# First loads, first splits and decay exponentials in another order, in a fused lightning-attention and router kernel

## The chip, the cores and the metric

The kernel runs on one core of a Trainium2 chip. The metric is the device time of one execution in microseconds (us), the median of three runs. A core has five engines with queues of their own: TensorE (PE in the profile; its weight loads are PEld), VectorE (DVE), ScalarE (ACT), GpSimd (POOL) and SyncE (SP), which here only issues DMAs. ACT issues some as well. Each engine takes its instructions strictly in the order in which the program lists them.

## The reference

Layer norm of x, a lightning-attention block s on it, a top-8 router block g on it, and x + s * silu(g). There are 2048 tokens of 512 features, read as four sequences of 512 by the kernel, 16 heads of 128, 64 experts.

```python
xn = _layernorm(x, axis=-1)
qkv = silu(einsum('bnf,of->bno', xn, w_qkv))       # q, k, v per head
q_decay = exp(-s * arr[:, None]); k_decay = exp(-s * (BLK - arr)[:, None])
diag_decay = where(idx >= 0, exp(-s * idx), 0.0);  block_decay = exp(-s * BLK)
# per block of tokens: o = (q * q_decay) @ kv + ((q k^T) * diag_decay) @ v
#                      kv = block_decay * kv + (k * k_decay)^T v
out = norm_w * (out * rsqrt(mean(out * out) + EPS))
s = einsum('bno,fo->bnf', sigmoid(einsum('bnf,of->bno', xn, w_gate)) * out, w_out)
logits = einsum('th,eh->te', flat, router_weight) + router_bias
topk_w, topk_idx = top_k(softmax(logits), 8)
g = silu(flat * sum(topk_w) + einsum('tk,tkh->th', topk_w, expert_bias[topk_idx]))
x = x + s * g
```

(`reshape` and the like are left out; `s` in the decays is the slope of the head.)

## The kernel before

**Tiles.** Tokens are cut into tiles of 128. The sequences go in two pairs p = 0, 1; a tile (p, t) means the t-th 128 tokens of both sequences of a pair, so two arrays x (128 x 512, float32). For each tile DVE takes mean and variance (`layer_norms`, L235: `bn_stats` L240, `bn_aggr` L241, add epsilon L242), POOL raises the variance to -1/2 (L246 or L250), DVE normalises in place (L216), PE transposes four 128 x 128 pieces per sequence into PSUM (`transpose`, L259), and the result is copied to `xf`.

**Split products.** Every large matrix product is done in float32r with operands split in two: a high half, which ACT casts (`split_hi`, L110), and a low half, source minus high half, which DVE or POOL subtracts (`split_lo`, L113). A product is three matmuls: high x high, high x low, low x high (`PASSES`). The products themselves follow a Strassen scheme with seven block products (`PRODUCTS`, L39): token blocks B11, B21, B22 and sums T1 to T4, weight blocks A11, A12, A22 and sums S1 to S4.

**The first stage.** It computes v for all heads in 16 units: `for k, (p, t) in enumerate(tiles + again)` (L1032), eight tiles with the first half of v's weights, `ws[0]`, then eight with `ws[1]`. Each is a `v_unit`. Units 0 and 1 are direct (`plain_unit`, L537): 8 block products of 6 matmuls, A11 with B11 and T1 (for a direct unit T1 holds the plain block b12), A12 with B21 and B22, then A21 and A22 with the same token blocks. The later ones use the Strassen scheme (`unit`, L498). A list `after` has seven places; what is put in place i is issued behind product i of the unit. In a direct unit, places 0, 1 and 2, 3 and 4, 5 and 6 come behind the products of A11, A12, A21 and A22. Through `after` a unit prepares the next tiles: `stats`, `norms`, `turn` (transposes, copies, and for p = 0 a store of `xf`), `sums`, `plain` and `more` (token blocks and their splits), `logits` (the router's 16 small matmuls, and one addition of the bias on DVE), and sums and splits of weights (`sum_of`, `split_one`).

**The start** is written out by hand (L985 to L1030). SP issues the loads: two x of tile (0,0), four weight blocks of `ws[0]`, two x of tile (0,1), four more weight blocks (`raw_v`, 256 KB each; two blocks make one of A11, A12, A21, A22). ACT issues five small loads (slope twice, router weight, router bias, norm weight) behind a table load for Exp. POOL makes the identity, and the distances for the decays (`make_dist`, L167). PE does `WARM` = 32 transposes of the identity. Then `make_decays` (L179): three exponentials on ACT and a memset on POOL. ACT loads the table for Silu (L1008). Then come the stats and norms of tile (0,0), its transposes, and the splits of unit 0 in the order of L1013 to L1030:

```python
pt = [transpose(stage, 0, j, 0, False) for j in range(PB)]
nc.vector.tensor_copy(xfs[0, 0][:, 0], pt[0])
split_hi(blocks[0, "B11"][:, 0, 0], pt[0][:, 0:KC])
ws[0].split_one("A11", nc.vector, hi=True)
```

with `logits(stage, 0, 0, [0])`, the router's matmuls for the first sequence, ahead of unit 0, and those of the second behind its first product.

**The decays** are made by row (`decay_row`), stored to DRAM by `keep_rows` (at unit 2) and spread to 128 partitions by `keep_decay`, one DMA per head, in units 13 to 15. The router's scores are exponentiated on ACT in unit 13 (`scores_exp`, L351). The attention behind the first stage reads both.

**Behind the first stage** come the units of gate and of q and k with the attention, the output projection and the final sum. The change touches nothing there.

PSUM: the transposes and the router's sums share a pool `ps_sc` of three banks, taken in turn.

Of the kernel before, what the change touches and what calls it, by code (L numbers as in the profile page):

```python
# [8 lines left out]
F32 = mybir.dt.float32  # L9
F32R = mybir.dt.float32r  # L10
AF = mybir.ActivationFunctionType
ALU = mybir.AluOpType
# [7 lines left out]
TOP_K = 8  # L20
LN_EPS = 1e-05
RMS_EPS = 1e-06
WARM = 32

# [36 lines left out]
def kernel(  # L61
# [44 lines left out]
    def tok(b, t):  # L106
        return bass.ds(b * N + t * P, P)
# [71 lines left out]
    def make_decays():  # L179
        nc.scalar.activation(decay_row, decay_row, AF.Exp, scale=slope_of)  # L180
        nc.scalar.activation(kdecay, slopes, AF.Exp, scale=rest_of)
        nc.scalar.activation(bdecay, slopes, AF.Exp, scale=-float(P))
        nc.gpsimd.memset(decay_row[:, 0 : P - 1], 0.0)

    def keep_rows():
# [40 lines left out]

    xts = {}

    def load_x(stage, b, t, bufs=None):
        xt = stage.tile([P, F], F32, tag="x", name=f"x_{b}_{t}", bufs=bufs)  # L230
        nc.sync.dma_start(out=xt, in_=x[tok(b, t), :])
        xts[b, t] = xt


    def layer_norms(p, t, apart=False):  # L235
        var = small.tile([P, PB], F32, tag="lnvar", name=f"lnv_{p}_{t}")
        for j in range(PB):
            b = p * PB + j
            st = small.tile([P, nc.vector.BN_STATS_DIM], F32, tag="bn", name=f"bn_{b}_{t}")
            nc.vector.bn_stats(st, xts[b, t])  # L240
            nc.vector.bn_aggr(stats[b][:, t, :], st)  # L241
            nc.vector.tensor_scalar(  # L242
                var[:, j : j + 1], stats[b][:, t, 1:2], 1.0, LN_EPS, ALU.mult, ALU.add
            )
            if apart:
                nc.gpsimd.tensor_tensor(  # L246
                    rstd_of[p][:, t, j : j + 1], var[:, j : j + 1], mhalf[:, 0:1], ALU.pow
                )
        if not apart:
            nc.gpsimd.tensor_tensor(rstd_of[p][:, t], var, mhalf[:, 0:PB], ALU.pow)  # L250
# [669 lines left out]
    NP_FIRST = 2  # L920

    def prepare(stage, p, t):
        first = (p, t) == (0, 0)
# [12 lines left out]
        def route_logits():  # L936
            logits(stage, p, t)
        return {
            "stats": lambda: layer_norms(p, t, first), "norms": lambda: normalise_x(p, t),
            "turn": turn, "sums": sums[0], "plain": sums[1], "more": sums[2], "logits": route_logits,  # L940
        }

# [39 lines left out]
    n1 = len(tiles)  # L982
    prep = [prepare(stage, p, t) for p, t in tiles]

    load_pair(stage, 0, 0)  # L985
    vloads = ws[0].load()
    vloads(4)
    load_pair(stage, 0, 1)
    vloads(4)
    make_first()  # L990

    nc.scalar.activation(kdecay[:, 0:NT], mhalf, AF.Exp)
    nc.scalar.dma_start(out=slope_of, in_=slope.rearrange("o h -> h o"))
    nc.scalar.dma_start(out=slopes, in_=slope.to_broadcast([P, NH]))
    nc.scalar.dma_start(out=rw, in_=router_w)
    nc.scalar.dma_start(out=rb, in_=router_b.to_broadcast([P, E]))
    nc.scalar.dma_start(out=nw, in_=norm_w)
    make_dist()
    sig = small.tile([P, NT], F32, tag="var", name="table")
    warm_up(WARM)  # L1000
    for i, n in enumerate(XN):
        block(0, i, xa if i < NX else xb, i)
        blocks[1, n] = blocks[0, n]
    for n in ["A21"] + [n for n, _, _, _ in PRODUCTS]:
        ws[0].place(n)
    make_decays()

    nc.scalar.activation(sig, mhalf, AF.Silu)  # L1008
    prep[0]["stats"]()
    prep[0]["norms"]()  # L1010

    pt = [transpose(stage, 0, j, 0, False) for j in range(PB)]
    nc.vector.tensor_copy(xfs[0, 0][:, 0], pt[0])  # L1013
# [12 lines left out]
    prep[1]["stats"]()  # L1026
    prep[1]["norms"]()
    ws[0].split_one("A21", nc.vector)
    load_pair(stage, *tiles[3])
    ws[0].split_one("A22", nc.gpsimd)  # L1030

    for k, (p, t) in enumerate(tiles + again):  # L1032
        g, after = k // n1, nothing()
        for unit_of, what in ((n1 - 3, (0, "top")), (n1 - 2, (0, "less")), (n1 + 2, (1, "top")), (n1 + 3, (1, "less"))):
            if k == unit_of:
                after[2].append(lambda what=what: scores_less(*what))
        if n1 - NT <= k < n1:
            after[6].append(lambda p=p, t=t: keep_blocks(p, t))
        if k + 1 < n1:
            after[0 if k else 1].append(prep[k + 1]["turn"])  # L1040
            if 0 < k < n1 - 3:
                after[0].append(lambda k=k: load_pair(stage, *tiles[k + 3]))
            if k == 0:
                after[1].insert(0, prep[2]["stats"])
            after[1].append(prep[k + 1]["sums"])
            if k + 2 < n1:
                if k:
                    after[1].append(prep[k + 2]["stats"])
                after[4 if k > 1 else 3].append(prep[k + 2]["norms"])
            after[1].append(prep[k + 1]["plain"])  # L1050
# [305 lines left out]
```

## Time and profile before

| what | value |
|---|---|
| median of 3 runs | 1055.41 us (1055.09 to 1055.75) |
| profiled execution, whole | 1056.31 us |
| its span (first to last instruction) | 1054.5 us |
| DVE, ACT, POOL busy | 638.3, 553.4, 682.0 us |
| granted TensorE clock | 1.00 throughout |
| DMA over the span | 185.12 MB, mean 176 GB/s |
| first warm-up transpose / first transpose of x | 1.38 / 7.39 us |
| first product of unit 0 / of unit 1 | 9.97 / 26.89 us |
| `scores_exp` in unit 13: table load / next Silu table load | 161.48 / 165.66 us |

Read the span as the time between the first and the last instruction; the execution's own time is some 1.8 us longer. "Busy" is the time in which an engine has an instruction of its own running; a wait shows as idle time before the instruction that waited, with the one that released it. SPq and ACTq lines are the issuing of DMAs, not the transfers.

### The profile page before, as it was taken

What the parts mean: (1) busy time and instruction counts of PE and PEld (TensorE: products, weight loads), DVE (VectorE), ACT (ScalarE), POOL (GpSimd) and SP (SyncE); (2) the same over time, 40 slices, a digit from 0 to 9 for tenths busy, and PEclk for the clock granted to TensorE, in tenths of its full rate; (3) what the DMA queues carried; (4) which work ended last, traced back from release to release, by engine and by line L of the source; (5) the groups of instructions that cost most, each with busy time, mean ns of one, the idle gap of its engine ahead of it and who ended that gap; (6) DMA issues with size and microseconds to landing.
All of it is one profiled execution on the core that took longest, in us unless ns stands there. A gap on an engine that the chain in (4) does not pass through costs nothing.

```text
span 1054.5 us, 17612 instructions
## 1 busy us (share of the span) xinstructions
PE 1044.0 (99%) x6338; PEld 925.0 (88%) x6338; DVE 638.3 (61%) x1017; ACT 553.4 (52%) x969; POOL 682.0 (65%) x698
## 2 busy tenths in 40 slices
PE   8999999999999999999999999999999999999997
PEld 7888888888888888888888888888888889999997
DVE  6675533347677676665554555555555458698767
ACT  5555554645545545555554555555545545574632
POOL 4887782768678777786777778877678643024023
PEclk9999999999999999999999999999999999999999
DMA  6456746544455455553854323633334236988863
GB/s 226 166 205 237 272 148 223 173 129 151 140 166 193 132 170 169 158 179 105 305 192 139 119 76 105 192 94 115 103 114 145 65 136 237 335 300 299 286 218 102
DMA packets 128838, 185.12 MB, mean 176 GB/s; under 512 B 11104, under 2 KB 72688, under 8 KB 127856
## 3 DMA queue, kind: packets, MB, share of 16 engines
q1 hardware_dynamic: 127856, 183.56, 53.1%
q8 instruction: 50, 0.82, 0.3%
q10 hardware_dynamic: 896, 0.44, 0.1%
q14 instruction: 36, 0.29, 0.1%
HBM read 115.26 MB, written 70.80 MB: 176 GB/s over the span
## 4 chain that ended last, share of the span: by engine, by line
PE 90%; DVE 4%; DMA 3%; ACT 1%; issue 1%; SPq 1%; POOL 0%; DVEq 0%; ACTq 0%; POOLq 0%
PE u_qk L516 27%; PE u_g L516 15%; PE u_v L516 13%; PE acc L1235 12%; PE sa L672 5%; PE o L757 5%; PE ss L695 4%; PE o L759 4%; PE kt L675 2%; PE d_v L546 1%; DMA raw_v<-in_w_v_dram 1%; PE lg L332 1%; DMA yin<-y 1%; ACT yr L110 1%; DMA raw_eb<-in_expert_b_dram 1%
## 5 line engine op out<-in xcount | busy, mean ns | idle before, releaser
L1235 PE MATMUL acc<-wr,yr 128*128 128x256 f32 x1344 | 163.4, 282 | 1.3 <-DVE a_o L900 1.3
L1235 PEld LDWEIGHTS acc<-wr,yr 128*128 128x128 f32 x1344 | 161.4, 190 | 3.3 <-DVE a_o L900 1.7
L516 PE MATMUL u_qk<-blk_T,ws_qk 128*128 128x512 f32 x576 | 141.6, 394 | 0.0
L769 POOL TENSOR_TENSOR sqs<-sqs,sq 128x512 f32<-128x512 f32 x60 | 79.1, 1318 | 94.9 <-ACT sq L768 94.9
L516 PEld LDWEIGHTS u_qk<-blk_T,ws_qk 128*128 128x128 f32 x576 | 107.0, 188 | 22.6
L113 POOL TENSOR_TENSOR ws_qk<-sum_qk,ws_qk 128x512 fp32r<-128x512 f32 x64 | 84.7, 1335 | 29.8 <-ACT ws_qk L110 29.8
L516 PE MATMUL u_qk<-blk_B,wa_qk 128*128 128x512 f32 x384 | 102.0, 401 | 0.0
L880 POOL TENSOR_TENSOR u<-u,x 128x256 f32<-128x256 f32 x28 | 33.4, 1213 | 99.5 <-DVE u L879 76.6
L113 DVE TENSOR_TENSOR yr<-yin,yr 128x1024 fp32r<-128x1024 f32 x56 | 75.6, 1354 | 35.5 <-ACT yr L110 35.4
L560 ACT ACTIVATE k<-k 128x512 f32<-128x512 f32 x64 | 40.5, 632 | 106.3 <-DVE k L507 106.3
L757 PE MATMUL o<-at,vin 128*128 128x128 f32 x512 | 88.5, 275 | 0.0
L516 PEld LDWEIGHTS u_qk<-blk_B,wa_qk 128*128 128x128 f32 x384 | 69.5, 189 | 14.5 <-ACT q L560 1.1
L110 ACT CAST yr<-yin 128x1024 fp32r<-128x1024 f32 x56 | 58.3, 1045 | 43.9 <-PE acc L1235 34.4
L761 DVE SCALAR_TENSOR_TENSOR y<-o,nw,gt 128x512 f32<-128x512 f32 x64 | 48.0, 751 | 49.9 <-PE o L759 49.9
L757 PEld LDWEIGHTS o<-at,vin 128*128 128x128 f32 x512 | 74.9, 192 | 2.5
L759 PE MATMUL o<-qd,st 128*128 128x128 f32 x384 | 74.3, 275 | 0.0
L768 ACT ACTIVATE sq<-o 128x512 f32<-128x512 f32 x60 | 35.9, 598 | 72.9 <-POOL sqs L769 41.7
L681 ACT ACTIVATE kd<-kt,kdecay 128x384 f32<-128x384 f32 x64 | 37.2, 581 | 67.9 <-PE kt L675 67.9
L516 PE MATMUL u_g<-blk_T,ws_g 128*128 128x512 f32 x288 | 72.4, 397 | 0.0
L699 DVE SCALAR_TENSOR_TENSOR st<-st,bdecay,ss 128x128 f32<-128x128 f32 x128 | 41.7, 346 | 44.2 <-ACT st L697 41.9
L672 PE MATMUL sa<-q,k 128*128 128x128 f32 x512 | 67.9, 276 | 0.3
L672 PEld LDWEIGHTS sa<-q,k 128*128 128x128 f32 x512 | 64.4, 191 | 3.8 <-ACT k L560 0.6
(199 smaller groups left out, 2405.6 us busy)
## 6 DMA issues: line engine op xcount, KB each, us to landing
yin<-y SPq DMA_DIRECT2D x56, 512.0 KB, 4.5
v<-vo_v SPq DMA_DIRECT2D x64, 256.0 KB, 2.8
raw_qk<-in_w_head_dram SPq DMA_DIRECT2D x64, 256.0 KB, 4.2
vin<-v SPq DMA_DIRECT2D x64, 256.0 KB, 3.6
y<-yS SPq DMA_DIRECT2D x64, 256.0 KB, 3.5
y<-y SPq DMA_DIRECT2D x48, 256.0 KB, 2.4
woin<-wo SPq DMA_DIRECT2D x18, 512.0 KB, 5.2
x<-in_x_dram SPq DMA_DIRECT2D x32, 256.0 KB, 4.6
```

The source lines that it names most:

```text
L110: nc.scalar.copy(hi, src)
L113: eng.tensor_tensor(lo, src, hi.bitcast(F32), ALU.subtract)
L516: nc.tensor.matmul(ps, lhsT, rhs, start=(first and c == 0 and n == 0), stop=(c == KC - 1 and n == len(PASSES) - 1), skip_group_check=not f ...
L560: nc.scalar.activation(dst, src, AF.Silu)
L672: nc.tensor.matmul(pa[:, c], k[:, c], q[:, c], start=True, stop=True)
L695: nc.tensor.matmul(ps[:, c], kd[s][:, c], v_of(b, h, c), start=True, stop=True)
L699: nc.vector.scalar_tensor_tensor(r[:, c], r[:, c - 1], bdecay[:, h : h + 1], ps[:, c], ALU.mult, ALU.add)
L757: nc.tensor.matmul(o, v_of(b, h, c), at[s][:, c], start=True, stop=(c == 0))
L759: nc.tensor.matmul(o, st[s][:, c - 1], qd[s][:, c - 1], start=False, stop=True)
L761: nc.vector.scalar_tensor_tensor(y, po, nw[:, h : h + 1], gts[s], ALU.mult, ALU.mult)
L769: nc.gpsimd.tensor_tensor(sq[b], sq[b], s1, ALU.add)
L1235: nc.tensor.matmul(acc[t // 2][:, t % 2], yr[:, yi, bass.ts(t, P)], wos[m, g // NQ][:, wi, g % NQ], start=(first and g == 0 and n == 0 and ...
```

## The change

- **Loads.** The second x of tile (0,0) is issued on ACT's queue. SP issues the first x, all eight weight blocks, the two x of tile (0,1), the router's weight and bias, and behind the first splits the slope loads and the norm weight. The x of tile (0,2) goes ahead of the store of `xf`.
- **Exponentials.** `make_decays` moves to unit 13, right ahead of `scores_exp`; its memset becomes `mask_decays`, in place 2 of that unit with `keep_rows`. The table load for Exp at the start goes. `keep_decay` starts two places later.
- **Start.** 24 warm-up transposes instead of 32, and the six others between the transposes of the two sequences. Stats, power and normalise of the two sequences are interleaved (`bn_of`). Splits are issued by halves of a weight block, in another order; A22's second low half goes from POOL to DVE.
- **Unit 0.** Tile (0,1)'s transposes and blocks and tile (0,2)'s stats move from place 1 to place 3, and all of tile (0,0)'s router matmuls to place 6.

```diff
-WARM = 32
+WARM = 24
...
+    def mask_decays():
         nc.gpsimd.memset(decay_row[:, 0 : P - 1], 0.0)
...
+    def load_x(stage, b, t, bufs=None, queue=None):
         xt = stage.tile([P, F], F32, tag="x", name=f"x_{b}_{t}", bufs=bufs)
+        (queue or nc.sync).dma_start(out=xt, in_=x[tok(b, t), :])
...
+    def bn_of(b, t):
+        p, j = b // PB, b % PB
+        st = small.tile([P, nc.vector.BN_STATS_DIM], F32, tag="bn", name=f"bn_{b}_{t}")
+        var = small.tile([P, PB], F32, tag="lnvar", name=f"lnv_{b}_{t}")
+
+        def power(j):
+            nc.vector.bn_aggr(stats[b][:, t, :], st)
+            nc.vector.tensor_scalar(
+                var[:, j : j + 1], stats[b][:, t, 1:2], 1.0, LN_EPS, ALU.mult, ALU.add
+            )
+            nc.gpsimd.tensor_tensor(
+                rstd_of[p][:, t, j : j + 1], var[:, j : j + 1], mhalf[:, 0:1], ALU.pow
+            )
+        return lambda: nc.vector.bn_stats(st, xts[b, t]), power
...
-    load_pair(stage, 0, 0)
-    vloads = ws[0].load()
-    vloads(4)
+    load_x(stage, 0, 0)
+    load_x(stage, 1, 0, queue=nc.scalar)
+    ws[0].load()(8)
     load_pair(stage, 0, 1)
-    vloads(4)
     make_first()
 
-    nc.scalar.activation(kdecay[:, 0:NT], mhalf, AF.Exp)
-    nc.scalar.dma_start(out=slope_of, in_=slope.rearrange("o h -> h o"))
-    nc.scalar.dma_start(out=slopes, in_=slope.to_broadcast([P, NH]))
-    nc.scalar.dma_start(out=rw, in_=router_w)
-    nc.scalar.dma_start(out=rb, in_=router_b.to_broadcast([P, E]))
-    nc.scalar.dma_start(out=nw, in_=norm_w)
+    sig = small.tile([P, NT], F32, tag="var", name="table")
+    nc.scalar.activation(sig, mhalf, AF.Silu)
+    nc.sync.dma_start(out=rw, in_=router_w)
+    nc.sync.dma_start(out=rb, in_=router_b.to_broadcast([P, E]))
     make_dist()
...
-    make_decays()
-
-    nc.scalar.activation(sig, mhalf, AF.Silu)
-    prep[0]["stats"]()
-    prep[0]["norms"]()
-
-    pt = [transpose(stage, 0, j, 0, False) for j in range(PB)]
+
+    first = [bn_of(b, 0) for b in range(PB)]
+    first[0][0]()
+    first[0][1](0)
+    first[1][0]()
+    normalise(xts[0, 0], xts[0, 0], 0, 0)
+    first[1][1](1)
+    pt = [transpose(stage, 0, 0, 0, False)]
+    warm_up(6)
     nc.vector.tensor_copy(xfs[0, 0][:, 0], pt[0])
+    normalise(xts[1, 0], xts[1, 0], 1, 0)
+    pt.append(transpose(stage, 0, 1, 0, False))
...
-    split_hi(blocks[0, "B11"][:, 0, 0], pt[0][:, 0:KC])
-    ws[0].split_one("A11", nc.vector, hi=True)
-    split_lo(nc.gpsimd, blocks[0, "B11"][:, 0, 1], b11, blocks[0, "B11"][:, 0, 0])
...
+    weights_hi("A11", 0)
+    tokens_hi("B11", pt[0][:, 0:KC])
+    weights_hi("A11", 1)
+    tokens_lo("B11", b11, nc.gpsimd)
+    weights_lo("A11", 0, nc.vector)
+    weights_lo("A11", 1, nc.vector)
+    weights_hi("A12", 0)
     nc.scalar.copy(xfs[0, 0][:, 1], pt[1])
+    load_pair(stage, *tiles[2])
     nc.sync.dma_start(out=xf_d[0], in_=xfs[0, 0])
-    load_pair(stage, *tiles[2])
-    warm_up(6)
-    split_blocks(0, 0, nc.vector, (("T1", b12), ("B21", b21), ("B22", b22)))
-    ws[0].split_one("A12", nc.vector, 0)
-    ws[0].split_one("A12", nc.gpsimd, 1)
-    logits(stage, 0, 0, [0])
+    tokens_hi("T1", b12)
+    tokens_lo("T1", b12, nc.vector)
+    tokens_hi("B21", b21)
+    weights_hi("A12", 1)
+    weights_lo("A12", 0, nc.vector)
+    weights_lo("A12", 1, nc.gpsimd)
+    tokens_lo("B21", b21, nc.vector)
+    tokens_hi("B22", b22)
+    tokens_lo("B22", b22, nc.vector)
+    ws[0].split_one("A21", nc.vector)
+    for i in range(2):
+        weights_hi("A22", i)
+    weights_lo("A22", 0, nc.gpsimd)
     prep[1]["stats"]()
+    weights_lo("A22", 1, nc.vector)
     prep[1]["norms"]()
-    ws[0].split_one("A21", nc.vector)
+    nc.sync.dma_start(out=slope_of, in_=slope.rearrange("o h -> h o"))
+    nc.sync.dma_start(out=slopes, in_=slope.to_broadcast([P, NH]))
+    nc.sync.dma_start(out=nw, in_=norm_w)
     load_pair(stage, *tiles[3])
-    ws[0].split_one("A22", nc.gpsimd)
...
         if k + 1 < n1:
-            after[0 if k else 1].append(prep[k + 1]["turn"])
+            early = 1 if k else 3
+            after[0 if k else 3].append(prep[k + 1]["turn"])
...
             if k == 0:
-                after[1].insert(0, prep[2]["stats"])
-            after[1].append(prep[k + 1]["sums"])
+                after[3].insert(0, prep[2]["stats"])
+            after[early].append(prep[k + 1]["sums"])
...
+            after[early].append(prep[k + 1]["plain"])
...
+            if k == 0:
+                after[6].append(lambda: logits(stage, 0, 0))
             after[4 if k else 6].append(prep[k + 1]["logits"])
-        if k == 0:
-            after[0].append(lambda: logits(stage, 0, 0, [1]))
...
-        if k == NP_FIRST:
-            after[0].append(keep_rows)
+        if k == n1 + NT + 1:
+            after[1] += [make_decays, scores_exp]
+            after[2] += [mask_decays, keep_rows]
         if n1 + NT < k < n1 + 2 * NT:
             for j in range(1, len(PRODUCTS)):
-                h = (k - n1 - NT - 1) * (len(PRODUCTS) - 1) + j - 1
-                if h < NH:
+                h = (k - n1 - NT - 1) * (len(PRODUCTS) - 1) + j - 3
+                if 0 <= h < NH:
                     after[j].append(lambda h=h: keep_decay(h))
-        if k == n1 + NT + 1:
-            after[1].append(scores_exp)
```

The helpers `weights_hi` and `weights_lo` split half i of a weight block (`bass.ts(i, width // 2)`), the first on ACT and the second on the engine given; `tokens_hi` and `tokens_lo` do the same for a token block of tile (0,0).

More of the change, by code (lines that the diff above doesn't have):

```diff
@@ L227, with layer_norms @@
     xts = {}
-    def load_x(stage, b, t, bufs=None):
+    def load_x(stage, b, t, bufs=None, queue=None):
         xt = stage.tile([P, F], F32, tag="x", name=f"x_{b}_{t}", bufs=bufs)
-        nc.sync.dma_start(out=xt, in_=x[tok(b, t), :])
+        (queue or nc.sync).dma_start(out=xt, in_=x[tok(b, t), :])
         xts[b, t] = xt
-    def layer_norms(p, t, apart=False):
+    def layer_norms(p, t):
         var = small.tile([P, PB], F32, tag="lnvar", name=f"lnv_{p}_{t}")
@@ L244, in layer_norms @@
             )
[L245 to L250, printed above, removed]
+        nc.gpsimd.tensor_tensor(rstd_of[p][:, t], var, mhalf[:, 0:PB], ALU.pow)
+    def bn_of(b, t):
[11 more added lines that the diff above has]
+        return lambda: nc.vector.bn_stats(st, xts[b, t]), power
     def normalise_x(p, t):
@@ L922, in prepare @@
     def prepare(stage, p, t):
-        first = (p, t) == (0, 0)
         def turn():
@@ L938, in prepare @@
         return {
-            "stats": lambda: layer_norms(p, t, first), "norms": lambda: normalise_x(p, t),
+            "stats": lambda: layer_norms(p, t), "norms": lambda: normalise_x(p, t),
             "turn": turn, "sums": sums[0], "plain": sums[1], "more": sums[2], "logits": route_logits,
@@ L983 @@
     prep = [prepare(stage, p, t) for p, t in tiles]
-    load_pair(stage, 0, 0)
-    vloads = ws[0].load()
-    vloads(4)
+    load_x(stage, 0, 0)
+    load_x(stage, 1, 0, queue=nc.scalar)
+    ws[0].load()(8)
     load_pair(stage, 0, 1)
-    vloads(4)
     make_first()
-    nc.scalar.activation(kdecay[:, 0:NT], mhalf, AF.Exp)
-    nc.scalar.dma_start(out=slope_of, in_=slope.rearrange("o h -> h o"))
-    nc.scalar.dma_start(out=slopes, in_=slope.to_broadcast([P, NH]))
-    nc.scalar.dma_start(out=rw, in_=router_w)
-    nc.scalar.dma_start(out=rb, in_=router_b.to_broadcast([P, E]))
-    nc.scalar.dma_start(out=nw, in_=norm_w)
+    sig = small.tile([P, NT], F32, tag="var", name="table")
+    nc.scalar.activation(sig, mhalf, AF.Silu)
+    nc.sync.dma_start(out=rw, in_=router_w)
+    nc.sync.dma_start(out=rb, in_=router_b.to_broadcast([P, E]))
     make_dist()
-    sig = small.tile([P, NT], F32, tag="var", name="table")
     warm_up(WARM)
@@ L1014, with weights_hi, weights_lo @@
+    pt.append(transpose(stage, 0, 1, 0, False))
     b11, b12, b21, b22 = halves(xfs[0, 0])
-    split_hi(blocks[0, "B11"][:, 0, 0], pt[0][:, 0:KC])
-    ws[0].split_one("A11", nc.vector, hi=True)
-    split_lo(nc.gpsimd, blocks[0, "B11"][:, 0, 1], b11, blocks[0, "B11"][:, 0, 0])
+    def weights_hi(n, i):
+        k, m = int(n[1]) - 1, int(n[2]) - 1
+        c = bass.ts(i, ws[0].width // 2)
+        split_hi(ws[0].of[n][:, 0, c], ws[0].raw[:, k, m, c])
+    def weights_lo(n, i, eng):
+        k, m = int(n[1]) - 1, int(n[2]) - 1
+        c = bass.ts(i, ws[0].width // 2)
+        split_lo(eng, ws[0].of[n][:, 1, c], ws[0].raw[:, k, m, c], ws[0].of[n][:, 0, c])
@@ L1018, with tokens_hi, tokens_lo @@
+    def tokens_hi(n, src):
+        split_hi(blocks[0, n][:, 0, 0], src)
+    def tokens_lo(n, src, eng):
+        split_lo(eng, blocks[0, n][:, 0, 1], src, blocks[0, n][:, 0, 0])
+    weights_hi("A11", 0)
[5 more added lines that the diff above has]
+    weights_hi("A12", 0)
     nc.scalar.copy(xfs[0, 0][:, 1], pt[1])
+    load_pair(stage, *tiles[2])
     nc.sync.dma_start(out=xf_d[0], in_=xfs[0, 0])
-    load_pair(stage, *tiles[2])
@@ L1049 @@
                 after[4 if k > 1 else 3].append(prep[k + 2]["norms"])
-            after[1].append(prep[k + 1]["plain"])
+            after[early].append(prep[k + 1]["plain"])
             after[4].append(prep[k + 1]["more"])
+            if k == 0:
+                after[6].append(lambda: logits(stage, 0, 0))
             after[4 if k else 6].append(prep[k + 1]["logits"])
-        if k == 0:
-            after[0].append(lambda: logits(stage, 0, 0, [1]))
         if k < NP_FIRST:
```

## The prediction

> **What bounds the kernel now.** I read the page's busy shares first, then who TensorE waits for, then the timeline of the first 27 us.
>
> ```profile
> PE 1044.0 (99%) x6338; PEld 925.0 (88%) x6338; DVE 638.3 (61%) x1017; ACT 553.4 (52%) x969; POOL 682.0 (65%) x698
> ...
> PE   8999999999999999999999999999999999999997
> ```
>
> TensorE fills the span but for its ends. Between 20 and 200 us its waits are one line:
>
> ```profile
> PE d_v L546 <- DVE w_A_v L113: 0.7, 1, 0.7
> ```
>
> It ends at 20.71; from there PE runs through. All this change can win or lose is therefore when PE gets through unit 0. My mark is the first matmul of unit 1, 26.89 before. The timeline up to it (start, length, engine, line, work, idle time before it and its releaser):
>
> ```profile
> 3.52 0.69 DVE L240 BATCH_NORM_STATS2 bn<-x 128x6 f32<-128x512 f32 x1 [3.52 <-DMA x<-in_x_dram]
> ...
> 4.46 0.15 DVE L242 TENSOR_SCALAR lnv<-stats 128x1 f32<-128x1 f32 x1
> ...
> 5.45 0.51 ACT L180 ACTIVATE decay_row<-decay_row,rest_of 16x256 f32<-16x256 f32 x1 [3.23 <-DMA x<-in_x_dram]
> ...
> 6.02 0.19 POOL L183 MEMSET decay_row<- 16x127 f32 x1 [3.42 <-ACT decay_row L180]
> ...
> 6.19 1.19 POOL L246 TENSOR_TENSOR rstd<-lnv,mhalf 128x1 f32<-128x1 f32 x2
> ...
> 6.79 1.16 DVE L216 TENSOR_SCALAR x<-x,stats,rstd 128x512 f32<-128x512 f32 x2 [0.68 <-POOL rstd L246]
> ...
> 8.81 0.37 ACT L110 CAST blk_B<-pt 128x256 fp32r<-128x256 f32 x1 [1.04 <-DVE xf L1013]
> ...
> 9.97 1.82 PE L546 MATMUL d_v<-w_A_v,blk_B 128*128 128x512 f32 x6
> ...
> 12.79 1.79 POOL L113 TENSOR_TENSOR w_A_v<-raw_v,w_A_v 128x512 fp32r<-128x512 f32 x1 [2.80 <-ACT w_A_v L110]
> ```
>
> ```profile
> 15.53 0.70 POOL L250 TENSOR_TENSOR rstd<-lnv,mhalf 128x2 f32<-128x2 f32 x1 [0.95 <-DMA raw_v<-in_w_v_dram]
> ...
> 17.03 3.08 POOL L113 TENSOR_TENSOR w_A_v<-raw_v,w_A_v 128x512 fp32r<-128x512 f32 x2 [0.80 <-ACT w_A_v L110]
> 17.19 3.47 DVE L113 TENSOR_TENSOR w_A_v<-raw_v,w_A_v 128x512 fp32r<-128x512 f32 x2
> ...
> 19.01 0.96 PE L546 MATMUL d_v<-w_A_v,blk_B 128*128 128x512 f32 x3 [0.50 <-DVE w_A_v L113]
> ...
> 20.71 0.51 PE L546 MATMUL d_v<-w_A_v,blk_B 128*128 128x512 f32 x1 [0.73 <-DVE w_A_v L113]
> ```
>
> To see: the first power (L246) was ready to start at 4.62 and ran at 6.19, behind a memset that waited for an exponential, which waited for a small load. Later PE waits for A21's low halves, which DVE and POOL made at once: two DVE subtractions took 3.47 where the shortest of this kind took 0.68.
>
> **The loads.** SP's own waits up to 45 us:
>
> ```profile
> SPq L432 <- DMA raw_v<-in_w_v_dram: 2.6, 1, 2.6
> ...
> SPq L432 <- DMA x<-in_x_dram: 0.9, 1, 0.9
> ```
>
> The third weight block issues at 3.51, when the first x (0.73 + 2.8) has landed; the fourth at 6.46, when the first block (1.63 + 4.8) has. Counting both queues, no more than eight loads are in flight. Four places went to small loads; afterwards the eight are two x and six weight blocks. The rate was 385 and 328 GB/s from 2.5 to 3.5 us, 134 to 232 in the next 2 us with the small loads among it, 360 after. I take 300 from 2.0 us on and 0.5 us for a landing: blocks 2, 4 and 8 at 6.0, 7.7 and 11.2, second x of tile 1 at 13.0. The low bound is 235 (236 and 233 in the windows 2 to 4 and 4 to 6): 7.0, 9.2, 13.7, 15.9. The second x, now first on ACT's queue, lands near 4.2 (4.97 before); sharing with it, the first lands near 3.8 (3.53).
>
> **Warm-up.** Transposes started every 0.213 us at 2.08, every 0.108 at 6.16, so 24 end near 6.3, not 7.3. Six more stand between the two tiles' transposes, where PE waits anyway.
>
> **Exponentials.** One table load (1.28), three exponentials (0.9 together) and the memset leave the start. Beside the router's they share its table load:
>
> ```profile
> 161.48 1.28 ACT L353 ACT_TABLE_LOAD   x1
> 162.78 1.15 ACT L353 ACTIVATE scores<-scores 128x512 f32<-128x512 f32 x2
> 165.66 1.28 ACT L560 ACT_TABLE_LOAD   x1 [1.73 <-issue]
> ```
>
> The 0.9 fits into the 1.73 that ACT idles; without that cover they cost at most 0.9. POOL is busy 0.60 of the 10 us there. On SP the row store now stands right ahead of the first row copy; it landed in 6.3 at 52, so SP may stand until 171 with v stores behind. Their buffers are wanted a unit (some 10 us) later: nothing, at worst about 1.
>
> **The new start, step by step** (durations from the rows; back-to-back DVE and ACT operations overlap by 0.08 to 0.1).
> - Stats of x0 from 3.82 to 4.92 (0.69, 0.18, 0.15 and gaps), power 0.57 to 5.56 while DVE does x1's 0.69, normalise 0.55 to 6.14. The warm-ups free PE at 6.3; transposes 0.65 to 7.0, DVE's copy 0.69 to 7.74, second normalise to 8.23, its transposes to 8.9. First product 8.95 instead of 9.97, with 8 router matmuls (0.9) moved behind the unit.
> - ACT: B11 after that copy, as at 8.81 before, to 8.14; A11's second half to 8.67; **half of A12**, for which block 4 must be in by 8.57, to 9.2; copy of xf 0.59, T1 0.41 to 10.1, B21, then the other half of A12 to 10.95, B22, A21 (1.04) to 12.2, A22's first half to 12.7.
> - DVE: A11's low halves to 9.83 (one POOL subtraction between), T1 to 10.57, A12's half to 11.17. At 11.03 POOL starts its half of A12 (1.38); B21 and B22 follow on DVE, to about 13.04. POOL takes A22's half at 12.85 for 1.35, so A21's first half ends at 14.78 and the second at 15.4. Stats of tile 1 (2.1) to 17.4, A22's last half to 18.0, power (0.70, held until 17.8) to 18.5, two normalises (1.0) to **19.5**. With no collision, the same operations end at **17.8**: A21 13.53, stats behind the landing 15.55, power 16.7.
> - PE: A11 and A12 products end at 15.25 (0.8 lost to B21's low half), A21 at 18.0. Tile 1's transposes, moved behind A21, then wait for the normalises: done at 20.0 instead of 18.9. A22's 12 matmuls 2.75, router 2 x 1.73: **26.25**. Gain 26.89 - 26.25 = **0.64 us**. What is late next is the normalise of tile 1, not a weight.
>
> Between the two ends, 19.5 and 17.8, I take the first: the rows nearest are the same subtractions of A21 and A22 side by side at 17.03 and 17.19, where one engine stood while the other worked. At the low load rate block 8 comes after A21's second subtraction and this collision falls away, but A12 and x are later: 19.1, gain 1.0.
>
> The Trainium skill, SBUF — State Buffer, section on the two separate sides, speaks against the change: VectorE operations with two SBUF inputs and GpSimd's share a port pair by an exclusive lock, held for the whole instruction. DVE's 1.77 at 17.19 (POOL's 1.38 from 17.03, then its own 0.68) agrees. By the rule the sum is the 0.64 above, and without it 2.3.
>
> **What moves on the queues.** SP: the router's weights and bias (2 issues of some 0.45) come behind tile 1's x, in by about 14 at 300 GB/s, wanted at 22.8. Tile 2's x goes ahead of the 512 KB store of tile 0's tokens; both wait for nothing later than ACT's copy at 9.7, and tile 2's stats on DVE begin at 20.6. The slope and norm loads (3 issues) are wanted at 161 and later. The load of tile 3 waits for tile 1's transposes, 20.0 instead of 17.62, and unit 0's v stores stand behind it; they have four buffers and the next unit needs them some 10 us on, so nothing, at worst the 2.4 of the delay. The Silu table load and its 0.2 now run under the wait for x; uncovered they would cost 1.5. Tile 1's prefetch, moved from step 1 to step 3 of unit 0, keeps A22 (2.75) and the router (3.46) between its transposes and unit 1: POOL writes its B11 at 24.1, PE wants it at 26.5, so nothing; a unit 1 without that cover would lose one for one.
>
> The router's matmuls are as many as before, 16 and 16. In the PSUM rotation one transpose of tile 2 now waits for DVE's addition of the first logits: about 28.9 against PE's 29.4, so nothing; if DVE is later, one for one. From unit 1 on the order is the old one, and POOL and DVE are ahead by about 1 us, so the gain lasts to the end.
>
> **Sum.** Span 1054.5 - 0.6 = 1053.9; with the 1.8 around it 1055.7 in an execution like the profiled one (1056.31). That one lies 0.9 above the median of 1055.41, so on the median's scale **1054.8**.
>
> **Rivals.**
> - *No collision* (chance 0.33). Tile 1 is normalised at 17.8, PE is through the transposes at 18.3 and at the mark at 24.55: gain 2.3, **1053.1**; with PE not waiting at all 2.7, 1052.7. For it: at 12.75 DVE went first and lost nothing to the POOL row at 12.79. Against: there no second two-input subtraction stood behind it on DVE; here five do.
> - *Tile 1's x too late* (0.20, the slower side). Its two loads now stand behind all eight weight blocks, before behind four. Normalise ends 3.2 after the landing (second stats 1.1, power held 0.35 and 0.70, normalises 1.0), so from a landing at 16.9 the gain is gone and each further us costs one. For it: an x issued at 11.65 took 6.8 to land. At the mean of the first 40 us, 202 GB/s, it lands at 18.1: **1056.6**; at the page's mean 176, at 20.4, 1058.9. Against: 300 and more while only large loads are queued.
> - *The small loads do not matter*: the power would still be early, as it waits for no load then; I give this no share of its own.
>
> **How the numbers follow.** The forecast, both collisions, has 0.47 and its own range 1054.3 to 1055.4. Measurements of this kernel can tell about 0.2% (2.1 us) from no change: faster means below 1053.3, which is most of the first rival and a tail of the forecast, 0.32; slower means above 1057.5, the worse half of the second, with what I overlook, 0.17; between, 0.51. The range 1052.7 to 1057.2 takes in the first rival to its floor and the second to three quarters of a us past its centre.
>
> **What would show it.** First power at 5.0, first product near 9; a POOL subtraction inside a long DVE one between 11 and 15.5; PE idle at 18 to 19 for the normalise of tile 1; unit 1 near 26.3; nothing idle on PE at 160 to 175. I am wrong if DVE's subtractions stay at 0.7 (then 1053.1), if ACT stands at A12 past 9.2, or if tile 1's x lands after 17. Page-only, and not in the sum: the Trainium skill's TensorE: Matmul & The Clock Gate, Part 1, says a pause of some 3.4 us halves PE's clock; no pause here should reach that.

## The result and the profile after

The changed kernel took 1057.07 us in the median of 11 executions (1055.77 to 1059.0), beside 1054.92 for the kernel before on the same chip (11 executions, 1053.25 to 1057.49). The ratio is 1.0021, with a 95% interval of 1.0014 to 1.0029. So it is slower by about 2.2 us, where 0.6 us of gain was forecast. Executions of one and the same kernel differ here by some us, so only ratios and rows of the trace are compared below.

The page of the changed kernel, its busy shares and TensorE's row of slices, looks as before:

```profile
PE 1043.3 (99%) x6330; PEld 924.0 (87%) x6330; DVE 638.4 (60%) x1018; ACT 552.4 (52%) x969; POOL 680.1 (64%) x697
...
PE   8999999999999999999999999999999999999997
```

TensorE's waits from 7 to 200 us are now three lines (engine, line, releaser: total us, times, longest):

```profile
PE pt L277 <- DVE x L218: 2.3, 3, 0.9
PE d_v L558 <- POOL blk_B L113: 0.3, 1, 0.3
PE d_v L558 <- DVE blk_B L113: 0.2, 1, 0.2
```

Of the first line 1.4 us lie ahead of the first product. Between it and unit 1 TensorE waits 0.31, 0.17 and 0.94 us. The timeline of the changed kernel (start, length, engine, line, work, count, idle time before it):

```profile
4.82 0.69 DVE L262 BATCH_NORM_STATS2 bn<-x 128x6 f32<-128x512 f32 x1 [4.82 <-DMA x<-in_x_dram]
...
6.00 0.57 POOL L259 TENSOR_TENSOR rstd<-lnv,mhalf 128x1 f32<-128x1 f32 x1 [3.40 <-DVE lnv L256]
...
8.96 1.82 DVE L113 TENSOR_TENSOR w_A_v<-raw_v,w_A_v 128x512 fp32r<-128x512 f32 x2
...
11.95 1.85 DVE L113 TENSOR_TENSOR blk_B<-xf,blk_B 128x256 fp32r<-128x256 f32 x2
13.72 2.38 DVE L113 TENSOR_TENSOR w_A_v<-raw_v,w_A_v 128x512 fp32r<-128x512 f32 x2
...
19.36 1.00 DVE L218 TENSOR_SCALAR x<-x,stats,rstd 128x512 f32<-128x512 f32 x2 [0.60 <-POOL rstd L247]
```

```profile
9.08 1.16 POOL L113 TENSOR_TENSOR blk_B<-xf,blk_B 128x256 fp32r<-128x256 f32 x1 [1.01 <-ACT blk_B L110]
11.87 1.31 POOL L113 TENSOR_TENSOR w_A_v<-raw_v,w_A_v 128x512 fp32r<-128x512 f32 x1 [1.63 <-ACT w_A_v L110]
13.65 1.30 POOL L113 TENSOR_TENSOR w_A_v<-raw_v,w_A_v 128x512 fp32r<-128x512 f32 x1 [0.46 <-ACT w_A_v L110]
```

```profile
9.52 0.47 PE L558 MATMUL d_v<-w_A_v,blk_B 128*128 128x512 f32 x1
10.30 1.45 PE L558 MATMUL d_v<-w_A_v,blk_B 128*128 128x512 f32 x5 [0.31 <-POOL blk_B L113]
...
19.96 1.18 PE L277 MATMUL pt<-ident,x 128*128 128x128 f32 x8 [0.94 <-DVE x L218]
20.89 2.98 PE L558 MATMUL d_v<-w_A_v,blk_B 128*128 128x512 f32 x12
23.71 3.68 PE L344 MATMUL lg<-rw,xf 128*128 128x64 f32 x32
27.20 1.64 PE L558 MATMUL d_v<-w_A_v,blk_B 128*128 128x512 f32 x6
```

To see: each of POOL's three subtractions stands beside a pair of DVE's, and each of these pairs is long. Unit 1 starts at 27.20. In the profiled execution of before that was 26.89, so this trace explains 0.3 of the 2.2 us. From there on the distance hardly changes: the output stage's first matmul comes at 871.45 here and at 871.08 before, 0.37 apart, and TensorE shows no wait from 160 to 200 us, where the exponentials now are. The remaining 1.9 us cannot be found in this pair of traces. (The time behind the output stage's first matmul differs between the traces of this case, from 182.1 to 185.0 us, so the kernels are compared at unit 1.)

### The profile page after: what moved, and what is told of

The parts are those of the page before. It is cut to its first block, busy times and chain, and to the rows that moved or that the text cites. A ratio compares the mean times of both kernels' runs of the same rounds, so it can differ in the third digit from the quotient of the medians.

```text
span 1056.5 us, 17594 instructions
## 1 busy us (share of the span) xinstructions
PE 1043.3 (99%) x6330; PEld 924.0 (87%) x6330; DVE 638.4 (60%) x1018; ACT 552.4 (52%) x969; POOL 680.1 (64%) x697
## 4 chain that ended last, share of the span: by engine, by line
PE 84%; DVE 7%; DMA 4%; issue 2%; ACT 1%; POOL 1%; SPq 0%; DVEq 0%; ACTq 0%; POOLq 0%
PE u_qk L528 27%; PE u_g L528 15%; PE u_v L528 11%; PE acc L1277 7%; PE sa L684 5%; PE o L769 5%; PE ss L707 4%; PE o L771 4%; DMA yin<-y 3%; PE kt L687 2%; DVE yr L113 2%; PE d_v L558 1%; PE lg L344 1%; DVE wr L113 1%; ACT yr L110 1%
```

## The experiments

In all tables and texts "the mark" is the first matmul of unit 1. Each experiment's mark is read from its own trace, its ratio is to the kernel before on the same chip in the same set of runs. "x lands" is the start of the first statistics, which wait for the first x. When the first ones were planned four things could have cost the time: the new order of the loads, the new order of the subtractions, the moved exponentials (theory C where a letter is used), and that the profiled execution of before was not a typical one (D).

| run | x lands | first product | mark | median, us | ratio (95%) |
|---|---|---|---|---|---|
| before, the profile shown | 3.52 | 9.97 | 26.89 | | |
| e0 before, profiled three times more | 3.44 to 3.58 | 9.74 to 9.91 | 24.92, 25.03, 24.99 | | |
| changed, the result | 4.82 | 9.52 | 27.20 | 1057.07 | 1.0021 (1.0014 to 1.0029) |
| e1 changed, again | 4.78 | 9.48 | 27.16 | 1056.13 | 1.0016 (1.0007 to 1.0025) |
| e2 both x on SP | 3.45 | 8.87 | 27.17 | 1056.13 | 1.0017 (1.0008 to 1.0025) |
| e4 exponentials back | 4.99 | 10.69 | 28.83 | 1057.74 | 1.0031 (1.0018 to 1.0043) |
| e3, e3b before, decays moved | 3.49, 3.46 | 9.71, 9.97 | 28.06, 27.16 | 1054.84 | 1.0003 (0.9990 to 1.0015) |
| e5 changed, no POOL subtraction | 4.33 | 9.03 | 25.11 | 1054.16 | 1.0000 (0.9992 to 1.0009) |
| e10 changed, A22's half alone to DVE | 4.33 | 9.03 | 25.64 | 1055.10 | 0.9998 (0.9987 to 1.0008) |
| e7 e5 with the logits back | 3.81 | 9.82 | 25.95 | 1055.12 | 1.0004 (0.9995 to 1.0013) |
| e8 before, A22 on DVE | 3.57 | 10.09 | 25.37 | 1053.50 | 0.9992 (0.9984 to 1.0001) |
| e6 e3, A22 on DVE | 3.41 | 10.18 | 25.44 | 1053.86 | 0.9995 (0.9986 to 1.0004) |
| e9 e6, 24 warm-ups | 3.52 | 9.62 | 24.46 | 1053.60 | 0.9989 (0.9980 to 0.9998) |

**e1: the changed kernel once more**, unaltered, for the spread of its start.

> The changed kernel unaltered, for a second profile. Theory A (a late first load): both x of tile (0,0) land near 4.8 to 5.0 us again, as in the first profile of the changed kernel (4.1 and 4.2 us after their issue at 0.73), and unit 1 begins near 27.2, some 0.3 us later than before (26.89); the rest of the 2 us by which the whole is slower is not at the start. Theory B (chance): the x land near 3.8 this time and unit 1 begins near 26.3. Time 1.0014 to 1.0029 of before by either.

Its start is the same row by row: the mark at 27.16, the pairs of DVE 1.83, 1.86 and 2.37 us. The loss is real and steady, 1.0016.

**e2: both x of tile (0,0) on SP.**

```diff
-    load_x(stage, 1, 0, queue=nc.scalar)
+    load_x(stage, 1, 0)
```

> The changed kernel with one edit: the second x of tile (0,0) is issued on SP behind the first, not on ACT. If two queues starting at once hold the first x back (theory A), the first x lands near 3.5 as before, its stats begin there instead of at 4.82, and unit 1 begins 0.5 to 1 us earlier than in the changed kernel, at 26.2 to 26.7; the time falls by the same, to about 1.001 of before. If the six weight blocks in flight hold it back, or the ramp of the DMA engines is slow by chance, it lands near 4.8 here too and unit 1 stays near 27.2.

The first x landed at 3.45, 1.4 us sooner, and the mark did not move, which neither branch of the expectation had. ScalarE's and TensorE's rows of this run say why:

```profile
7.92 0.62 ACT L110 CAST w_A_v<-raw_v 128x512 fp32r<-128x512 f32 x1 [5.70 <-DMA raw_v<-in_w_v_dram]
```

```profile
8.87 0.50 PE L558 MATMUL d_v<-w_A_v,blk_B 128*128 128x512 f32 x1 [0.48 <-ACT blk_B L110]
9.90 1.42 PE L558 MATMUL d_v<-w_A_v,blk_B 128*128 128x512 f32 x5 [0.53 <-POOL blk_B L113]
```

A11's two blocks were in at 7.9, against 6.5 in the changed kernel, and their cast began there: what x gained the weight lost, and B11's cast stands behind it on ACT. From B21's subtraction at 11.9 on, the two runs are the same. So the late x is not what costs the time.

**e4: the exponentials back at the start**, with their two loads on ACT's queue, all else as changed.

```diff
+    nc.scalar.activation(kdecay[:, 0:NT], mhalf, AF.Exp)
+    nc.scalar.dma_start(out=slope_of, in_=slope.rearrange("o h -> h o"))
+    nc.scalar.dma_start(out=slopes, in_=slope.to_broadcast([P, NH]))
...
+    make_decays()
+    nc.scalar.activation(sig, mhalf, AF.Silu)
     first = [bn_of(b, 0) for b in range(PB)]
...
```

> The changed kernel with the exponentials back at the start (two slope loads on ACT's queue, table load for Exp, three exponentials, memset behind the second power, row store at unit 2). Theory A: ACT has until about 8.6 before it is needed, so unit 1 begins within 0.5 us of the changed kernel's 27.2, and the time stays 1.0014 to 1.0029 of before. Theory C: the time falls by 1 to 2 us towards 1.000, with unit 1 no earlier.

It got worse: mark 28.83, ratio 1.0031. The exponentials waited for their loads (`slopes` at 7.94), the Silu table came at 8.36, and the casts of A11 began at 9.77. DVE's first subtraction came at 10.40 instead of 8.96, and tile 1 was normalised at 21.99 instead of 20.36. So moving them away is a gain in this order, not the cause of the loss. (The granted clock was 0.50 from 11.63 to 15.04 in this trace; tile 1's transposes, at 21.59, come right behind DVE's first normalise all the same.)

**e3: the kernel before, with the decays alone moved**, and profiled a second time (e3b).

```diff
...
-    make_decays()
-
...
+        if k == n1 + NT + 1:
+            after[1] += [make_decays, scores_exp]
+            after[2] += [mask_decays, keep_rows]
...
```

> The kernel before with the decays' exponentials, their memset and the row store moved to unit 13 and nothing else; the early small loads stay. Theory A (the move is free): the first power runs at 4.7 instead of 6.19, PE is still held by 32 warm-ups to 7.3, unit 1 begins at 26.4 to 26.9, and the time is 0.9990 to 1.0003 of before. Theory C (the move costs what the start does not explain): unit 1 as early, but the time is 1.001 to 1.002 of before, and PE or the queue of SP shows a wait behind 160 us that is not there before.

> The kernel before with only the exponentials moved to unit 13, once more. Its runs spread from 1052.57 to 1057.64, and its first profile was of the slowest, with unit 1 at 28.07. Theory D: in a run near 1053 unit 1 begins at 24.5 to 25.5. Theory T: at 28 again.

The ratio is unclear, 1.0003, and its executions scatter from 1052.57 to 1057.64. The profiles fell on late marks, 28.06 and 27.16, and what makes both late is a pair of rows that no other kernel had for tile 1 (e3, POOL's and DVE's rows):

```profile
15.72 2.68 POOL L113 TENSOR_TENSOR w_A_v<-raw_v,w_A_v 128x512 fp32r<-128x512 f32 x2
15.79 2.90 DVE L218 TENSOR_SCALAR x<-x,stats,rstd 128x512 f32<-128x512 f32 x2 [0.82 <-POOL rstd L252]
```

A22's blocks came in two us sooner than before (cast at 14.40, against 16.56 in e0b below), POOL, which goes on to A22 right behind its own power, was ahead of DVE by 0.07 us, and DVE's two normalises, 1.00 us for this tile in the other kernels, took 2.90 (in e3b 0.08 us and 2.90). The order of two starts this close decides over 1.9 us. That e3's mark is 0.9 us behind e3b's has another cause: up to A21's products e3 was ahead (19.24 against 19.89), but its granted clock was 0.50 from 19.19 to 22.61, and A21's first six matmuls took 2.91 us instead of the 1.63 of e3b, whose clock stayed at 1.00. The Trainium skill, SBUF — State Buffer, in its section on who interferes with whom, says that issue order decides who blocks, and that VectorE's tensor-scalar form can take the shared pair too; the 2.90 agrees.

**e0: the kernel before, unaltered, profiled three times more** (e0a, e0b, e0c), all for the question that e0a's expectation puts.

> The kernel before, unaltered, for another profile. Its profiled execution took 1056.31 us, its runs on the second chip 1052.71 to 1057.22 with a median of 1054.15, so that one may not be typical. Theory D (the baseline profile had a slow start): in an execution near 1053 to 1054 unit 1 begins near 25, not at 26.89, because a wait for A21's low halves or for a load is absent; then the change loses 2 us at the start and all of the difference is explained there. Theory T (the tail): unit 1 begins at 26.9 again and the executions differ only behind 870 us, in the output stage with its DMA waits; then the change's 2 us are mostly not made at the start.

All three marks are near 25.0, not 26.89, in executions of 1054.13, 1053.24 and 1054.67 us. ACT's, DVE's and POOL's rows of e0b:

```profile
16.56 1.05 ACT L110 CAST w_A_v<-raw_v 128x1024 fp32r<-128x1024 f32 x1 [0.34 <-DMA raw_v<-in_w_v_dram]
```

```profile
17.15 1.29 DVE L113 TENSOR_TENSOR w_A_v<-raw_v,w_A_v 128x512 fp32r<-128x512 f32 x2
```

```profile
17.69 3.17 POOL L113 TENSOR_TENSOR w_A_v<-raw_v,w_A_v 128x512 fp32r<-128x512 f32 x2 [1.49 <-ACT w_A_v L110]
```

Here A22's block landed later, POOL began 0.54 us behind DVE instead of 0.16 ahead of it, and A21's two subtractions took 1.29 us instead of 3.47. TensorE's only wait from 7 to 200 us in this run is 0.2. The profile that the prediction was made from was of the rarer kind: four traces of before have 26.89 once and 25.0 three times.

**e5: the changed kernel, all of the first unit's subtractions on DVE.**

```diff
-    tokens_lo("B11", b11, nc.gpsimd)
+    tokens_lo("B11", b11, nc.vector)
...
-    weights_lo("A12", 1, nc.gpsimd)
+    weights_lo("A12", 1, nc.vector)
...
-    weights_lo("A22", 0, nc.gpsimd)
     prep[1]["stats"]()
+    weights_lo("A22", 0, nc.vector)
```

> The changed kernel, with the three subtractions of the first unit that GpSimd makes (the low half of B11, one half of A12, one half of A22) given to VectorE, so that in the first 22 us no GpSimd subtraction stands beside one of VectorE. Theory of the collisions: of the 2.2 us by which unit 1 starts later than in the plain executions of the kernel before (27.2 against 25.0), 1.4 us are TensorE's waits (0.31, 0.17 and 0.94) for blocks and tokens that the shared side of the memory made late. VectorE takes over 0.43 + 0.69 + 0.69 = 1.8 us, but its pairs fall from 1.82, 1.85 and 2.38 to 1.3, 0.85 and 1.3 us; tile 1 is normalised by 19.1 instead of 20.36, and unit 1 starts at 25.8 to 26.2: some 1.2 us below the changed kernel, a ratio to the kernel before of 1.0003 to 1.0012. The rival, that the order of the work alone made it later, has VectorE's chain longer by up to 1.8 us: unit 1 at 27.2 or later, ratio 1.0016 or more.

DVE's and TensorE's rows of this run:

```profile
8.54 0.43 DVE L113 TENSOR_TENSOR blk_B<-xf,blk_B 128x256 fp32r<-128x256 f32 x1
8.88 1.29 DVE L113 TENSOR_TENSOR w_A_v<-raw_v,w_A_v 128x512 fp32r<-128x512 f32 x2
...
12.05 0.75 DVE L113 TENSOR_TENSOR blk_B<-xf,blk_B 128x256 fp32r<-128x256 f32 x2
12.73 1.28 DVE L113 TENSOR_TENSOR w_A_v<-raw_v,w_A_v 128x512 fp32r<-128x512 f32 x2
...
17.27 1.00 DVE L218 TENSOR_SCALAR x<-x,stats,rstd 128x512 f32<-128x512 f32 x2
```

```profile
17.88 1.17 PE L277 MATMUL pt<-ident,x 128*128 128x128 f32 x8
...
25.11 1.64 PE L558 MATMUL d_v<-w_A_v,blk_B 128*128 128x512 f32 x6
```

DVE does three subtractions more and is done sooner: tile 1 is normalised by 18.27 instead of 20.36. The waits of 0.31, 0.17 and 0.94 are gone, and the loss with them (1.0000). Of the 2.09 us by which the mark moved, 0.49 is an x that landed sooner in this execution; from first product to mark it is 16.08 us against 17.68, so the collisions cost **1.6 us**. The mark came out 0.7 below the expected range: x accounts for most of that. The ratio, 1.0000 with ±0.0009, is below its range as well, if not clear of it.

**e10: only A22's half to DVE**, B11's and A12's left on POOL (the third hunk above alone).

> The changed kernel with GpSimd's half of A22 alone given to VectorE, behind tile 1's statistics; the halves of B11 and A12 stay on GpSimd. If each collision counts by itself: A21's pair falls from 2.38 to 1.3, tile 1's statistics start at 14.9 (with x landed as in the changed kernel, 4.8) instead of 16.0, both halves of A22 lie in the wait for the power, tile 1 is normalised at 19.3 instead of 20.36, TensorE's wait for it falls from 0.94 to 0.2 or less and the other two (0.31, 0.17) stay: unit 1 at 26.2 to 26.6, ratio to the kernel before 1.0006 to 1.0014. If the collisions only count together, or A22 comes late now, unit 1 stays at 27.0 or later, ratio 1.0015 or more.

DVE's and TensorE's rows:

```profile
13.22 1.28 DVE L113 TENSOR_TENSOR w_A_v<-raw_v,w_A_v 128x512 fp32r<-128x512 f32 x2
```

```profile
9.80 1.42 PE L558 MATMUL d_v<-w_A_v,blk_B 128*128 128x512 f32 x5 [0.30 <-POOL blk_B L113]
...
18.41 1.14 PE L277 MATMUL pt<-ident,x 128*128 128x128 f32 x8
...
25.64 1.64 PE L558 MATMUL d_v<-w_A_v,blk_B 128*128 128x512 f32 x6
```

From first product to mark 16.61 us: A22's half alone costs 17.68 - 16.61 = 1.07, the other two 0.53. The collisions count one by one. The mark was to be 26.2 to 26.6; less the 0.49 of the sooner x that is 25.7 to 26.1, and 25.64 was measured. The ratio, 0.9998 with ±0.001, is below the expected range and says no more than that most of the loss is gone.

**e7: e5 with the eight logit matmuls of the first half back ahead of the first product**, B11's cast first, both x on SP, the router's weight and bias on ACT's queue at the start.

```diff
...
+    tokens_hi("B11", pt[0][:, 0:KC])
+    logits(stage, 0, 0, [0])
     weights_hi("A11", 0)
-    tokens_hi("B11", pt[0][:, 0:KC])
...
```

> The changed kernel with no GpSimd subtraction in the first unit (as in the run with all on VectorE), both tokens on SyncE's queue, the router's weights on ScalarE's queue from the start, the eight logit matmuls of tile 0's first half back ahead of the first product, and B11's cast ahead of A11's. Theory of two causes (collisions 1.4 us, logits moved out of an idle gap of TensorE 1.0 us): the first product starts at 8.5 to 8.9, TensorE is busy for 15.3 us from there with at most 0.6 of waits, so unit 1 starts at 24.0 to 24.8, ahead of the kernel before; ratio 0.9985 to 0.9998. If only the collisions count, 25.0 to 25.5 and a ratio of 1.0000 to 1.0005. If the small loads at the start hold up the tokens or A11, the first product comes after 9.5 and unit 1 after 25.3.

A miss, the third case of the expectation: the small loads held A11 up. ACT's and TensorE's rows:

```profile
9.14 1.14 ACT L110 CAST w_A_v<-raw_v 128x512 fp32r<-128x512 f32 x2 [1.02 <-DMA raw_v<-in_w_v_dram]
```

```profile
8.72 1.00 PE L344 MATMUL lg<-rw,xf 128*128 128x64 f32 x8
9.82 1.92 PE L558 MATMUL d_v<-w_A_v,blk_B 128*128 128x512 f32 x6
...
23.36 2.79 PE L344 MATMUL lg<-rw,xf 128*128 128x64 f32 x24
```

A11's two blocks were in at 9.1, 1.2 us later than in e2, whose loads differ only by these 160 KB (one trace of each). That moving the logits out of the gap costs is seen in the size: 24 of them behind the unit take 2.79, 32 take 3.68, so eight are 0.89. What they would bring with A11 in time was not measured.

**e8, e6, e9: the kernel before without its collision.** In e8 only A22's two subtractions go to DVE; e6 moves the decays as well; e9 also has 24 warm-ups.

```diff
-    ws[0].split_one("A22", nc.gpsimd)
+    ws[0].split_one("A22", nc.vector)
```

> The kernel before with A22's two subtractions on VectorE behind A21's. Theory of the collisions: the late start of unit 1 in the profiled execution (26.90 against 24.93 to 25.03 in three others) is left out for good: A21's pair takes 1.29 us in every execution, unit 1 starts at 24.9 to 25.1, and the median falls by the share of executions that collide times 1.9 us: ratio 0.9985 to 0.9999. The rival: VectorE, with 1.3 us more, makes A22 late for its products at 20.6 and delays tile 2's statistics; unit 1 at 25.5 or later, ratio 1.0002 or more.

> The kernel before with the decays' exponentials moved (as in the run of the decays alone), and A22's two subtractions on VectorE behind A21's instead of on GpSimd. Theory of the collisions: the two profiles of the decays alone had unit 1 at 28.07 and 27.16 because GpSimd's A22 began 0.07 us ahead of VectorE's normalising of tile 1 and held it for 2.90 instead of 1.00 us; without GpSimd's pair the normalising takes 1.00 and unit 1 starts at 24.6 to 25.1; ratio 0.9985 to 1.0000. The rival, that the later loads of the decays or the missing exponentials move something else, keeps unit 1 at 27 or later and the ratio at 1.0003 or more.

> The kernel before with the decays' exponentials moved, A22's two subtractions on VectorE, and 24 warm-up matmuls instead of 32. In the run with 32 the two powers came at 4.59 and 6.15 already, but TensorE's warm-ups ran to 8.0 and the transposes began at 7.84. With 24 they end by 6.6, the transposes begin at 7.0 to 7.4, the first product at 9.5 to 9.8 instead of 10.19, unit 1 at 24.8 to 25.1 instead of 25.45; ratio 0.9983 to 0.9998. If the casts' wait for A11's block sets the first product instead (it landed at 6.5 in the changed kernel, at 7.9 with both tokens on one queue), there is no gain: 10.0 and 25.3, ratio as in the run with 32 (0.9995).

e8's executions lie between 1052.94 and 1054.78, before's beside them between 1053.13 and 1057.98: the long ones are gone. Its mark, 25.37, is above the expected 25.1; the first product came at 10.09, from where it is 15.28 us, as the 15.29 in e0b. e6's mark, 25.44, is above its range too: it had its first power at 4.59 instead of some 6.1, and gained nothing by it, since the 32 warm-ups held TensorE until 8.0. With 24 (e9, TensorE's rows) they don't:

```profile
6.66 0.66 PE L267 MATMUL pt<-ident,x 128*128 128x128 f32 x4
...
9.62 1.63 PE L548 MATMUL d_v<-w_A_v,blk_B 128*128 128x512 f32 x6
...
24.46 1.64 PE L548 MATMUL d_v<-w_A_v,blk_B 128*128 128x512 f32 x6
```

e9's mark is 0.3 below what was expected. e9 is faster than the kernel before, by 0.11% (0.02 to 0.20%, so only just clear of no change), and faster than the changed one. It keeps two parts of the change, the decays and the 24 warm-ups, and leaves out the rest.

## Why the prediction was wrong

**The step that failed is the first one: "My mark is the first matmul of unit 1, 26.89 before", and with it the close of the sum, "That one lies 0.9 above the median of 1055.41, so on the median's scale 1054.8".** It took the 0.9 for something that both kernels carry. But the very wait that the prediction showed, for A21's low halves at 19.01 and 20.71, is not there in the other three traces of before: of the 2.3 us by which the profiled execution (1056.31) is longer than these three on average, 1.9 are there. Their marks average 24.98, 1.9 us below the mark that the gain was counted from. (A21's two low halves are both DVE's; what POOL made beside them was A22's, not A21's as the prediction has it.) Against 24.98 the forecast's own mark, 26.25, is a loss of 1.3 us, and the measured one, 27.2, a loss of 2.2 us, which is the measured 0.21%. The loss is complete there: the output stage's first matmul comes at 869.17 to 869.27 in the three traces and at 871.45 in the changed kernel, again 2.2 apart. So of the 2.8 us between forecast and measurement 1.9 are the zero and 0.95 the mark itself. That 1057.07 lies inside the outer range, below 1057.2, is no merit of the forecast: that part of it stood for tile 1's x landing late.

Where the 2.2 comes from, between the three plain traces of before and the changed kernel:

- First product 9.52 against 9.83: 0.3 gained.
- First product to mark 17.68 against 15.15: 2.5 lost. Of this the collisions are 1.6 (e5), and the eight logit matmuls, which had stood ahead of the first product in a gap, 0.9 (their size in e7; 16.08 - 15.15 in e5 gives the same; no run puts them back alone, so this part is counted, not tested).

Point by point, the rest of the prediction:

- **The collisions** were right in place, kind and size: a pair of POOL's and DVE's subtractions at A11, A12 and A22, at 1.7 between its two ends (19.5 and 17.8) and 1.6 as measured. The rule that the prediction cites from the Trainium skill, SBUF — State Buffer, section on the two separate sides, held here too: beside POOL's row at 13.65 DVE's first subtraction of A21 took 1.78 and behind it the second 0.68 in the changed kernel.
- **The loads** were wrong by 1 us at one place. x was to land at 3.8 and landed at 4.8, A11's second block at 6.44 as about reckoned (6.0), tile 1's second x at 12.31 instead of 13.0. The later rows are late by 0.6 to 1.0: first power 6.00 instead of 5.0, first product 9.52 instead of 8.95, A11's low halves done at 10.78 instead of 9.83, tile 1 normalised 20.36 instead of 19.5, the mark 27.20 instead of 26.25. With x sooner the mark would still be late: e2 had the x at 3.45, and A11's blocks took its place as the bound.
- **The exponentials** at unit 13 cost nothing, as forecast: ACT's loads and exponentials take 161.81 to 167.27 there, and TensorE waits for nothing from 160 to 200.
- **Warm-ups**: 24 ended at 6.43, forecast 6.3. What eight fewer are worth once the power is early, e6 against e9 show: 0.56 us at the first product.
- **The logits** were in the sum, at 0.9. They were no term of the difference there, since the mark of before was that of a run in which TensorE waited anyway.
- **The clock.** In the changed kernel it was granted in full from 5.94 us on. In e3 and e4 it fell to 0.50 for 3.4 us, and TensorE's longest pauses before that were 1.04 and 1.51 us; e3b had pauses as long as e3's (1.06 and 0.79) and kept 1.00. So a single pause of some 3.4 us, as in the prediction's last sentence, is not needed for it.
- **The rivals.** *No collision* is nearest to what e5 built: its mark, 25.11, came where that rival put 24.55, 0.6 later, 0.5 of it by the x (4.33, not 3.82), but the gain of 2.3 did not come, since the kernel before has no such wait in three of its four traces. *Tile 1's x too late* falls: that x was in at 12.31, and DVE came to it at 16.02. The slower side came by a mechanism that was in the forecast all along, measured from a wrong zero.

Left open: how often the kernel before collides. Of its 33 executions in one set six were above 1056 us, but the time behind 871 us scatters by up to 2.9 us too, so the times alone don't say.

## What to carry to other kernels

A wait that one profile shows between two engines that start within some tenths of a us of each other may be absent in most executions; before a gain is counted from such a wait, compare two or three more profiles of the unaltered kernel. Where DVE and POOL both have subtractions of two SBUF inputs, giving all to DVE can end sooner than sharing them (here tile 1 was normalised at 18.27 instead of 20.36, 0.49 of it by an x that landed sooner). And when the first load is moved ahead, ask which load then comes last, since the sum of what must be in hardly changes (e2: x sooner by 1.4 us, A11 later by 1.4).

## What the runs showed of the hardware that was not expected

- Two engines' starts 0.07 to 0.54 us apart decide over 1.9 us: POOL ahead by 0.16 (before, shown) or 0.07 (e3), and DVE's pair took 3.47 (subtractions) or 2.90 (normalises); DVE ahead by 0.17 to 0.54 (e0), and its subtractions took 1.29.
- The normalise, which reads one tile and two columns of scalars, is held by a POOL subtraction as the subtractions are (2.90 instead of 1.00), the statistics beside POOL's row at 12.31 in e3 are not (0.69).
- Where the first two loads are issued at 0.73 on two queues (the changed kernel, e1, e4, e5, e10), the first x was in at 4.33 to 4.99 and the chip moved 147 to 263 GB/s from 2.0 to 3.5 us; with both on SP (all other traces) it was in at 3.41 to 3.81, at 255 to 316 GB/s. Why is open.
- The granted clock fell to 0.50 for 3.4 us in e3 (from 19.19) and e4 (from 11.63), with no pause of TensorE above 1.51 us ahead of it.
